# Moving a query scale into the softmax: eight short exponentials per tile on ScalarE

## The chip, the cores and the metric

The kernel runs on one core of a Trainium2 chip. The core has five engines with a queue each: TensorE (PE, matrix products; PEld are its weight loads), VectorE (DVE), ScalarE (ACT), GpSimd (POOL) and SyncE (SP, which only issues DMAs here). Each takes its instructions in order and waits on semaphores for the others. The time is that of one launch on the device, in microseconds (us); the median of several runs is compared.

## The reference

Four stages, each with a layernorm and a residual: a state-space layer ("mamba"), a routed expert layer, a dynamic convolution, and six layers of a local-attention transformer with a feed-forward part. Input is 4 sequences of 1024 tokens, 128 wide, float32. The change lies in the attention:

```python
q = l2norm(q) * qs
k = l2norm(k) * ksc
q = q * cos * scale + rotate_half(q) * sin * scale
k = k * cos * inv + rotate_half(k) * sin * inv
...
sim = jnp.einsum('bhwie,bhwje->bhwij', bq, bk2) * QK_SCALE
sim = jnp.where(mask, -jnp.finfo(sim.dtype).max, sim)
attn = jax.nn.softmax(sim, -1)
out = jnp.einsum('bhwij,bhwje->bhwie', attn, bv2)
```

There are 16 heads of 64; a window of 32 queries looks at 64 keys (its own window and the one before). `l2norm` divides a head's vector by its length. Since that is one number per query and head, it can be applied to the vector or, later, to the row of scores.

## The kernel before, in words

The transformer works on tiles of 128 tokens: 4 sequences, 6 layers, 8 tiles each, 192 in all. The loop in `Transformer.run` (L1501) takes one tile per turn and lists several parts of neighbouring tiles in it: the scores of tile i, the mixing of tile i - 1, the projection of tile i + 2 and a step of a feed-forward, beside steps of the first three stages for later sequences.

`project` (L1256) makes queries and keys of a tile. Four products of 512 columns go to PSUM banks named `qk`; ScalarE squares them, VectorE multiplies by cosine (to `r`) and by sine (to `rb`) and sums the squares. GpSimd adds `rb` to `r`. From the sums of squares `inverse_root` (L559) makes `root`, one over the length, for 16 query heads and 16 key heads; its helper operands are kept in `words`, a PSUM bank. Then, in L1296 to L1302, GpSimd multiplies `r` by `root`, first for the queries and then for the keys.

`turn` (L1314) transposes both on TensorE. `scores` (L1328) fills two banks named `sim`, one with the scores of the even heads (e = 0) and one of the odd heads, 8 heads x 64 keys each. The mask is put into the bank ahead of them, as 0 or -1e30. For each bank VectorE takes the row maximum `mx` and writes score minus maximum to `at` in SBUF, which empties the bank. One ScalarE exponential of 1024 columns covers both; VectorE sums, and GpSimd divides. `mix` (L1387) transposes the weights (`aT`), multiplies with the tokens (`zT`), and with the value and output weights (`wvo`).

The order on every engine is computed ahead by a planner, `Order.arrange` (L278). Each call is recorded in `take` (L170) as a unit with an engine, an estimated cost (`length`, L248) and its dependencies; a `together` block makes one unit of several calls at a given cost, so that nothing comes between. `arrange` gives out the unit that can start first, and among those of one engine that could start within a small tolerance (`NEAR`, 0.25 us for ScalarE) the one listed first. It chooses among 7 banks, held from the unit that first writes to the last that reads. A unit whose activation table differs from the last one costs 1.28 us more. For VectorE operations with two SBUF inputs (`both`, L196) there is a rule:

```python
                    if u.both:
                        t = max(t, clock["gpsimd"])
                    elif e == "gpsimd":
                        t = max(t, locked)
```

In the plan, such an operation starts when GpSimd has ended what it has been given, and GpSimd's next one waits for it. All instructions are issued from one helper, `give` (L369), so that the profile puts them at line 374: they are told apart by the names of their tiles.

Of the kernel before, what the change touches and what calls it, by code (L numbers as in the profile page):

```python
# [10 lines left out]
F32 = mybir.dt.float32  # L11
BF16 = mybir.dt.bfloat16
I32 = mybir.dt.int32
AF = mybir.ActivationFunctionType
ALU = mybir.AluOpType
AX = mybir.AxisListType
PSUM = bass.MemoryType.PSUM

P = 128
# [38 lines left out]
class Late:  # L58
# [4 lines left out]
    def __init__(self, bank, make=lambda ap: ap):  # L63
        self.bank, self.make = bank, make
# [80 lines left out]
class Order:  # L145
# [16 lines left out]
    def bank(self, name):  # L162
        return Late(Bank(self.psum[0], name))

    def together(self, cost):
        return Together(self, cost)

# [218 lines left out]


class Together:  # L390
    def __init__(self, order, cost):
        self.order, self.cost = order, cost

    def __enter__(self):
        o = self.order
        o.open = Unit("tensor", len(o.units))
        o.open.side = o.side
        o.units.append(o.open)
        o.forced = self.cost
# [750 lines left out]
class Transformer:  # L1150
# [4 lines left out]
    def __init__(self, ctx, c):  # L1155
        self.c, self.nc, self.io = c, c.nc, c.io
        one = self.sb = c.sb
        self.mask = one.tile([P, 2, 64], BF16, name="mask")
        self.identb = one.tile([P, P], BF16, name="identb")
        self.lng = one.tile([P, DEPTH], F32, name="lng")  # L1160
        self.lnb = one.tile([P, DEPTH], F32, name="lnb")
        self.b1 = one.tile([P, 2, 3, DEPTH], F32, name="b1")
        self.b2 = one.tile([P, DEPTH], F32, name="b2")
        self.maskf = one.tile([P, 2, 64], F32, name="maskf", tag="exsT", bufs=2)
        self.wvod = [c.dram.tile([P, 2, 8, D], F32, name=f"wvod{l}") for l in range(DEPTH)]
        self.rotd = [c.dram.tile([P, TPB, 4, DH], F32, name=f"rotd{l}") for l in range(DEPTH)]
        self.w, self.rot = {}, {}

    def prepare(self):

# [85 lines left out]
    def project(self, i, b, t):  # L1256

        nc, c = self.nc, self.c
        lhs = c.hs[b][0][:, PRE + t * P : PRE + (t + 1) * P]
        full, half = [P, HEADS, DH], [P, HEADS // 2, DH]  # L1260
        rs = []
        rot = self.rot.pop(i)
        w = c.tiny()
        ss = w[:, :32]
        for s in range(2):
            r = self.sb.tile(full, F32, "r", tag=f"r{s}", bufs=2)
            rb = self.sb.tile(full, F32, "rb", bufs=2)
            for j in range(2):
                hd = slice(8 * j, 8 * j + 8)
                ps = c.bank("qk")  # L1270
                nc.tensor.matmul(
                    ps, lhs, self.w["qk", s][:, j * 512 : (j + 1) * 512], start=True, stop=True
                )
                pv = ps.rearrange("p (h d) -> p h d", d=DH)
                sq = self.sb.tile(half, F32, "sq", bufs=2)
                nc.scalar.activation(sq, pv, AF.Square)
                cos, sin = rot[:, 2 * s, None, :], rot[:, 2 * s + 1]
                nc.vector.tensor_tensor(
                    out=r[:, hd, :], in0=pv, in1=cos.to_broadcast(half), op=ALU.mult
                )  # L1280
                nc.vector.tensor_tensor(
                    out=rb[:, hd, :].rearrange("p h (k d) -> p h k d", k=2),
                    in0=swapped(ps),
                    in1=sin.rearrange("p (k d) -> p k d", k=2)[:, None].to_broadcast(
                        [P, HEADS // 2, 2, DH // 2]
                    ),
                    op=ALU.mult,
                )
                c0 = s * HEADS + 8 * j
                nc.vector.tensor_reduce(out=ss[:, c0 : c0 + 8], in_=sq, op=ALU.add, axis=AX.X)  # L1290
            nc.gpsimd.tensor_tensor(out=r, in0=r, in1=rb, op=ALU.add)
            rs.append(r)
        root = self.sb.tile([P, 32], F32, "root", bufs=3)
        nc.vector.tensor_scalar(root, ss, 1e-24, None, ALU.max)
        c.inverse_root(root, root, w[:, 32:])
        for s in range(2):  # L1296
            nc.gpsimd.tensor_tensor(
                out=rs[s],
                in0=rs[s],
                in1=root[:, s * HEADS : (s + 1) * HEADS, None].to_broadcast(full),  # L1300
                op=ALU.mult,
            )  # L1302
        return rs

    def keys(self, prev_k):
# [19 lines left out]
                nc.scalar.copy(dst[:, 4 * j : 4 * j + 4, :], pt)  # L1325
        return qT

    def scores(self, t, qT, kT):  # L1328

        nc, c = self.nc, self.c
        m = self.mask[:, 0 if t == 0 else 1, None, :].to_broadcast([P, 8, 2 * WIN])
        sv = [c.bank("sim").rearrange("p (a k) -> p a k", k=2 * WIN) for e in range(2)]
        with nc.together(2.0):
            for e in range(2):
                nc.tensor.matmul(
                    sv[e], self.identb, m, start=True, stop=False, skip_group_check=True
                )
            for a in range(8):  # L1340
                for g in range(4):
                    for e in range(2):
                        rows = slice(e * 64, (e + 1) * 64)
                        cols = slice(g * WIN, (g + 1) * WIN)
                        nc.tensor.matmul(
                            sv[e][cols, a, :],
                            qT[rows, a, cols],
                            kT[rows, a, g * WIN : (g + 2) * WIN],
                            start=False,
                            stop=True,  # L1350
                            skip_group_check=True,
                        )
        mx = self.sb.tile([P, 2, 8], F32, "mx", bufs=3)
        at = self.sb.tile([P, 8, 2, 2 * WIN], F32, "at", bufs=2)
        for e in range(2):
            nc.vector.tensor_reduce(out=mx[:, e, :], in_=sv[e], op=ALU.max, axis=AX.X)
            nc.vector.tensor_tensor(
                out=at[:, :, e, :],
                in0=sv[e],
                in1=mx[:, e, :, None].to_broadcast([P, 8, 2 * WIN]),  # L1360
                op=ALU.subtract,
            )
        av = at.rearrange("p a e k -> p (a e) k")
        nc.scalar.activation(av, av, AF.Exp)
        sm = self.sb.tile([P, HEADS], F32, "sm", bufs=3)
        nc.vector.tensor_reduce(out=sm, in_=av, op=ALU.add, axis=AX.X)
        nc.vector.reciprocal(sm, sm)
        nc.gpsimd.tensor_tensor(
            out=av, in0=av, in1=sm[:, :, None].to_broadcast([P, HEADS, 2 * WIN]), op=ALU.mult
        )  # L1370
        return at
# [129 lines left out]
    def run(self):  # L1501
# [44 lines left out]
        kT = self.keys(None)  # L1546
        at = xw = None
        coming = going = None
        for i in range(len(tiles) + 4):
            mixing = iter(())  # L1550
            if i < len(tiles):
                b, l, t = tiles[i]
                qT = self.turn(projected.pop(i), kT)
            if going and going[4] == 1:
                next(going[0])
            if 0 < i <= len(tiles):
                bm, lm, tm = tiles[i - 1]
                mixing = self.mix(bm, tm, at, xw if tm else None)
                xw = next(mixing)
            along(i, 0.25)  # L1560
            second = going and going[4] == 1
            if going:
                next(going[0])
            if i < len(tiles):
                at = self.scores(t, qT, kT)
                kT = self.keys(kT if t + 1 < TPB else None)
            if second:
                next(going[0], None)
                bf, jf, lf = going[1:4]
                if lf == DEPTH - 1:  # L1570
                    self.output(bf, jf)
                if jf == BPB - 1 and i < len(tiles):
                    self.load_ffn((lf + 1) % DEPTH)
            along(i, 0.5)
            next(mixing, None)
            if going and not second:
                next(going[0])
            along(i, 0.75)
            if not second:
                ahead(i + 2)  # L1580
            next(mixing, None)
            if second:
                ahead(i + 2)
                going = None
            elif going:
                next(going[0])
                going[4] = 1
            if 0 < i <= len(tiles):
                if tm == TPB - 1 and i < len(tiles):
                    self.load_vo((lm + 1) % DEPTH)  # L1590
                if tm % 4 == 3:
                    going = [self.feedforward(bm, tm // 4, lm), bm, tm // 4, lm, 0]
            along(i, 1)
# [137 lines left out]
```

## Time and profile before

| | |
|---|---|
| median of 3 runs (lowest to highest) | 4260.55 us (4259.56 to 4266.35) |
| the profiled execution: time, span | 4259.06 us, 4257.2 us |
| mean granted TensorE clock | 0.948 of full speed |
| VectorE `at<-bank,mx`, 128x512, 384 times | 682 ns each, 254.6 us |
| VectorE sum `sm<-at`, 128x1024, 192 times | 1211 ns each, 232.5 us |
| GpSimd `r<-r,rb`, 128x1024, 384 times | 2367 ns each, 906.9 us |
| GpSimd `at<-at,sm`, 128x1024, 192 times | 1903 ns each, 365.4 us |
| ScalarE copy `zT<-bank`, 128x512, 768 times | 597 ns each, 403.7 us |
| ScalarE table loads, 195 times | 1283 ns each, 250.2 us |

A row of the groups reads: line, engine, operation, written tile <- read tiles, shapes, number | busy us in all, mean ns of one | idle us of that engine just before them, and what ended most of it. A row of waits reads: who waited <- for whom: us in all, times, longest. Busy shares are means over stretches with different limits; the slices show where each engine is full. A busy TensorE isn't TensorE at its peak: the ends of its products are modelled.

### The profile page before, as it was taken

To read this page: it belongs to the slowest core of one execution; us is meant where nothing else is said; L and a number is where in the kernel's file an instruction comes from. 1 tells how busy PE (TensorE), PEld (TensorE's weight loads), DVE (VectorE), ACT (ScalarE), POOL (GpSimd) and SP (SyncE) were. 2 spreads that over 40 slices of the span, in tenths; PEclk is the share of its full clock that TensorE was granted. 3 is DMA by queue.
4 is the path that set the end of the run, shared out by engine and by line. 5 is a ranking of instruction groups with operands and counts; after the bars stand their busy time and mean duration, and the time that the engine had idled before them with its cause. 6 is when DMAs were issued, how large, how long until landed. Compare 5 with 4: busy or idle time off the path is not lost. (4 is left out here: it accounts for less than half of the span.)

```text
span 4257.2 us, 112033 instructions
## 1 busy us (share of the span) xinstructions
PE 3801.6 (89%) x45306; PEld 2721.5 (64%) x45317; DVE 3612.4 (85%) x9374; ACT 2610.7 (61%) x4854; POOL 2964.5 (70%) x1832
## 2 busy tenths in 40 slices
PE   3874788998988999988999999999999999999997
PEld 1762465675665666656676677766666777777775
DVE  4668789888997879999998787898989898888985
ACT  3754466675555777655667676666665666666664
POOL 3388667666878766777789665788688666666663
PEclk6886899999998999989999999999999999999998
DMA  3323321222112221111113122121111010101100
GB/s 91 104 83 123 119 85 43 86 62 72 60 68 82 91 73 55 45 57 53 44 63 114 58 65 63 41 73 59 58 61 51 27 41 25 32 21 34 33 27 11
DMA packets 136878, 261.25 MB, mean 61 GB/s; under 512 B 16112, under 2 KB 93992, under 8 KB 129192
## 3 DMA queue, kind: packets, MB, share of 16 engines
q1 hardware_dynamic: 123352, 211.47, 15.0%
q0 software_dynamic: 13008, 42.62, 3.2%
q8 instruction: 357, 5.85, 0.6%
q14 instruction: 161, 1.32, 0.1%
HBM read 224.41 MB, written 29.62 MB: 60 GB/s over the span
## 5 line engine op out<-in xcount | busy, mean ns | idle before, releaser
L374 POOL TENSOR_TENSOR r<-r,rb 128x1024 f32<-128x1024 f32 x384 | 906.9, 2367 | 365.2 <-DVE rb L374 297.9
L374 POOL TENSOR_TENSOR r<-r,root 128x1024 f32<-128x1024 f32 x384 | 723.2, 1903 | 181.2 <-DVE root L374 154.4
L374 PE MATMUL bank<-wqk,hs 128*128 128x512 f32 x1536 | 769.7, 624 | 45.0 <-DVE at L374 13.3
L374 PEld LDWEIGHTS bank<-zT,wvo 128*128 128x128 f32 x6144 | 723.2, 194 | 88.8 <-issue 53.2
L374 PE MATMUL bank<-zT,wvo 128*128 128x128 f32 x6144 | 729.4, 277 | 6.5 <-ACT zT L374 3.5
L374 ACT ACTIVATE sq<-bank 128x512 f32<-128x512 f32 x768 | 450.4, 601 | 458.1 <-DVE words L374 228.1
L374 ACT COPY zT<-bank 128x512 f32<-128x512 f32 x768 | 403.7, 597 | 382.4 <-PE bank L374 376.6
L374 DVE TENSOR_TENSOR r<-bank,rot 128x512 f32<-128x512 f32 x768 | 522.0, 680 | 103.4 <-issue 36.2
L374 POOL TENSOR_TENSOR at<-at,sm 128x1024 f32<-128x1024 f32 x192 | 365.4, 1903 | 326.2 <-DVE sm L374 146.3
L374 DVE TENSOR_TENSOR rb<-bank,rot 128x512 f32<-128x512 f32 x768 | 520.8, 678 | 62.8 <-ACT sq L374 53.8
L374 DVE TENSOR_REDUCE words<-sq 128x8 f32<-128x512 f32 x768 | 526.5, 686 | 14.3 <-ACT sq L374 5.3
L374 PEld LDWEIGHTS bank<-wqk,hs 128*128 128x128 f32 x1536 | 267.6, 195 | 322.7 <-issue 157.7
L374 PE MATMUL bank<-aT,xw 64*128 64x256 f32 x3072 | 430.6, 404 | 25.4 <-DVE at L374 10.3
L374 PE MATMUL bank<-ident,r 128*128 128x128 f32 x3080 | 400.6, 278 | 45.1 <-DVE rb L374 10.0
L374 PEld LDWEIGHTS bank<-ident,r 128*128 128x128 f32 x3080 | 350.1, 143 | 134.9 <-issue 59.7
L374 PEld LDWEIGHTS bank<-aT,xw 64*128 64x128 f32 x3072 | 295.6, 192 | 153.2 <-issue 44.3
L374 PEld LDWEIGHTS bank<-kT,qT 64*32 64x32 f32 x24576 | 259.7, 106 | 106.8 <-issue 105.4
L374 PE MATMUL bank<-kT,qT 64*32 64x64 f32 x24576 | 296.6, 227 | 12.4 <-issue 11.9
L374 DVE TENSOR_REDUCE mx<-bank 128x8 f32<-128x512 f32 x384 | 254.1, 680 | 44.4 <-PE bank L374 44.3
L374 PE MATMUL bank<-fxn,w 128*128 128x512 f32 (+1 forms) x576 | 272.8, 607 | 7.0 <-ACT fxn L374 4.8
L374 ACT ACTIVATE at<-at 128x1024 f32<-128x1024 f32 x192 | 203.5, 1060 | 117.6 <-DVE at L374 83.2
L374 ACT COPY qT<-bank 128x512 f32<-128x512 f32 x384 | 228.3, 600 | 66.2 <-PE bank L374 62.8
(207 smaller groups left out, 6849.8 us busy)
## 6 DMA issues: line engine op xcount, KB each, us to landing
near<-rows SPq DMA_DIRECT2D x31, 1024.0 KB
near<-rows SPq DMA_DIRECT2D x31, 960.0 KB
rot<-rotd SPq DMA_DIRECT2D x192, 128.0 KB
wqk<-in_Wqkv SPq DMA_DIRECT2D x48, 512.0 KB
wvo<-wvod SPq DMA_DIRECT2D x24, 1024.0 KB
ewt<-in_w_ex SPq DMA_DIRECT2D x16, 514.0 KB
w<-in_W SPq DMA_DIRECT2D x24, 341.0 KB
wvod<-eT SPq DMA_DIRECT2D x24, 256.0 KB
```

What stands on the lines that cost most here:

```text
L374: getattr(engine, op)(*map(real, args), **{k: real(v) for k, v in kw.items()})
```

## The change

The queries of the even heads are no longer multiplied by their root. GpSimd multiplies only the odd query heads and all key heads. In the softmax of the even heads VectorE takes the maximum of the unscaled scores and makes minus maximum times root from it; ScalarE then computes exp(root x score - root x maximum) straight from the bank, one instruction of 64 columns per head, with root as its scale and the product as its bias. The eight are listed as two units of four, each booked at 1.12 us. The odd heads keep their subtraction and get an exponential of their own, of 512 columns. The ring of root tiles grows from 3 to 5.

```diff
-    def together(self, cost):
-        return Together(self, cost)
+    def together(self, cost, engine="tensor"):
+        return Together(self, cost, engine)
...
 class Together:
-    def __init__(self, order, cost):
-        self.order, self.cost = order, cost
+    def __init__(self, order, cost, engine):
+        self.order, self.cost, self.engine = order, cost, engine
...
-        o.open = Unit("tensor", len(o.units))
+        o.open = Unit(self.engine, len(o.units))
...
-        self.w, self.rot = {}, {}
+        self.w, self.rot, self.roots = {}, {}, {}
...
-        root = self.sb.tile([P, 32], F32, "root", bufs=3)
+        root = self.sb.tile([P, 32], F32, "root", bufs=5)
         nc.vector.tensor_scalar(root, ss, 1e-24, None, ALU.max)
         c.inverse_root(root, root, w[:, 32:])
-        for s in range(2):
-            nc.gpsimd.tensor_tensor(
-                out=rs[s],
-                in0=rs[s],
-                in1=root[:, s * HEADS : (s + 1) * HEADS, None].to_broadcast(full),
-                op=ALU.mult,
-            )
+
+        qo = rs[0].rearrange("p (a e) d -> p a e d", e=2)[:, :, 1, :]
+        ro = root[:, :HEADS].rearrange("p (a e) -> p a e", e=2)[:, :, 1:2]
+        nc.gpsimd.tensor_tensor(
+            out=qo, in0=qo, in1=ro.to_broadcast([P, HEADS // 2, DH]), op=ALU.mult
+        )
+        nc.gpsimd.tensor_tensor(
+            out=rs[1], in0=rs[1], in1=root[:, HEADS:, None].to_broadcast(full), op=ALU.mult
+        )
+        self.roots[i] = root
         return rs
...
-    def scores(self, t, qT, kT):
+    def scores(self, i, t, qT, kT):
...
-        for e in range(2):
-            nc.vector.tensor_reduce(out=mx[:, e, :], in_=sv[e], op=ALU.max, axis=AX.X)
-            nc.vector.tensor_tensor(
-                out=at[:, :, e, :],
-                in0=sv[e],
-                in1=mx[:, e, :, None].to_broadcast([P, 8, 2 * WIN]),
-                op=ALU.subtract,
-            )
+        even = self.roots.pop(i)[:, :HEADS].rearrange("p (a e) -> p a e", e=2)[:, :, 0]
+        nc.vector.tensor_reduce(out=mx[:, 0, :], in_=sv[0], op=ALU.max, axis=AX.X)
+        nc.vector.scalar_tensor_tensor(mx[:, 0, :], mx[:, 0, :], -1.0, even, ALU.mult, ALU.mult)
+        for a0 in (0, 4):
+            with nc.together(1.12, "scalar"):
+                for a in range(a0, a0 + 4):
+                    nc.scalar.activation(
+                        at[:, a, 0, :],
+                        sv[0][:, a, :],
+                        AF.Exp,
+                        bias=mx[:, 0, a : a + 1],
+                        scale=even[:, a : a + 1],
+                    )
+        nc.vector.tensor_reduce(out=mx[:, 1, :], in_=sv[1], op=ALU.max, axis=AX.X)
+        nc.vector.tensor_tensor(
+            out=at[:, :, 1, :],
+            in0=sv[1],
+            in1=mx[:, 1, :, None].to_broadcast([P, 8, 2 * WIN]),
+            op=ALU.subtract,
+        )
+        nc.scalar.activation(at[:, :, 1, :], at[:, :, 1, :], AF.Exp)
         av = at.rearrange("p a e k -> p (a e) k")
-        nc.scalar.activation(av, av, AF.Exp)
```

More of the change, by code (lines that the diff above doesn't have):

```diff
@@ L1564, in run @@
             if i < len(tiles):
-                at = self.scores(t, qT, kT)
+                at = self.scores(i, t, qT, kT)
                 kT = self.keys(kT if t + 1 < TPB else None)
```

## The prediction

> **What bounds the kernel now.** I read the page's busy line first, then its slices, then the groups of the softmax, then what TensorE waited for, and last the order of time around one softmax.
>
> ```profile
> PE 3801.6 (89%) x45306; PEld 2721.5 (64%) x45317; DVE 3612.4 (85%) x9374; ACT 2610.7 (61%) x4854; POOL 2964.5 (70%) x1832
> ...
> PE   3874788998988999988999999999999999999997
> ...
> DVE  4668789888997879999998787898989898888985
> ACT  3754466675555777655667676666665666666664
> PEclk6886899999998999989999999999999999999998
> ```
>
> TensorE is busy for 89% of the span, but not evenly. Summing the stretches: from 0 to 532 us it is busy 338.3 us (start-up), from 532 to 3325 us 2569.8 of 2793 (92%), from 3325 to 4123 us 784.2 of 798 (98%). After 532 us only 262 us of TensorE idle are left. Any gain must come out of them; a loss has no such cap. What ended these waits, from 532 us to the end:
>
> ```profile
> PE bank L374 <- DVE at L374: 37.0, 37, 5.2
> PE bank L374 <- DVE rb L374: 28.5, 35, 4.9
> PE bank L374 <- ACT fxn L374: 24.8, 28, 4.5
> ...
> PE bank L374 <- ACT qT L374: 13.6, 21, 1.4
> ...
> PE bank L374 <- ACT zT L374: 12.6, 24, 1.2
> ...
> PE bank L374 <- POOL r L374: 7.1, 8, 2.4
> ```
>
> Added up by engine: VectorE 129 us, ScalarE 79 us, GpSimd 13 us. The first two rows are PSUM banks that TensorE wanted back: `at` is the subtraction that empties a score bank, `rb` the rotation that empties a projection bank.
>
> **The change, part by part.** A tile is 128 tokens; there are 192. The rows as they stand now:
>
> ```profile
> L374 POOL TENSOR_TENSOR r<-r,root 128x1024 f32<-128x1024 f32 x384 | 723.2, 1903 | 181.2 <-DVE root L374 154.4
> ...
> L374 DVE TENSOR_REDUCE mx<-bank 128x8 f32<-128x512 f32 x384 | 254.1, 680 | 44.4 <-PE bank L374 44.3
> ...
> L374 ACT ACTIVATE at<-at 128x1024 f32<-128x1024 f32 x192 | 203.5, 1060 | 117.6 <-DVE at L374 83.2
> ```
>
> GpSimd: half of the query multiply goes. The row is 1903 ns for 1024 columns; the same kind of multiply with 496 columns (`ew<-ew,csm`) took 1022 ns. So 1903 - 1022 = 0.88 us less per tile, 169 us in all. The chain of waits shows the query multiply and the key multiply in series ahead of the transposes, once per layer in the last stretch, but TensorE's whole wait for `r` is 7.1 us: worth at most that; I take 5 us. All else there is behind other work.
>
> VectorE: one subtraction of 682 ns goes, one `scalar_tensor_tensor` over 8 columns comes. Nearest row by size: the same operation on 4 columns takes 150 ns. That is a gain of 0.53 us per tile, 102 us, if nothing blocks it. But both its tensors (`mx` and the roots) lie in SBUF. The inverse root avoids this by keeping one operand in PSUM. What two SBUF inputs cost is in the trace, where the router's small operations meet GpSimd (order of time, start and length in us; first row GpSimd):
>
> ```profile
> 2138.38 4.71 POOL L374 TENSOR_TENSOR r<-r,rb 128x1024 f32<-128x1024 f32 x2
> ...
> 2141.11 2.06 DVE L374 TENSOR_TENSOR ehot<-rank,ebest 128x64 f32<-128x64 f32 x1
> ```
>
> The same operation takes 0.21 us when GpSimd is idle; here it ends at 2143.17, just after GpSimd's pair ends at 2143.09. The Trainium skill, page "SBUF — State Buffer", section "Who interferes with whom", has the rule: a VectorE instruction with two SBUF inputs takes a read port shared with GpSimd, and the later one is blocked for the whole instruction of the other. It speaks against this change. By the rule alone, an arrival at random finds GpSimd busy 0.65 of the time (0.70 less the part removed) with on average half of some 2 us left: 0.65 us, so VectorE would lose 0.65 - 0.53 = 0.12 us per tile. The measured row is nearer to a planned instruction:
>
> ```profile
> L374 DVE SCALAR_TENSOR_TENSOR m<-m,dpar,m 128x512 f32<-128x512 f32 x7 | 9.0, 1286 | 0.0
> ```
>
> Without contention it is 751 ns (its one twin on `r`), so the mean stall is 0.53 us, though the planner holds such an operation until its GpSimd clock is free, as it will the new one. Bounds: 0 and 2.37 us (the longest common GpSimd operation). I take 0.53: VectorE's gain is used up, 0 us. A blocked VectorE also holds up what is queued behind it: the reduction of the odd heads, and the rotations that empty projection banks.
>
> ScalarE: one exponential of 1060 ns goes; one of 512 columns and eight of 64 come. For 512 columns from SBUF the row `m<-m` gives 0.63 us. For 64 columns with scale and bias read per partition the nearest row is the layernorm:
>
> ```profile
> 3779.47 1.53 ACT L374 ACTIVATE fxn<-bank,mean,rs 128x128 f32<-128x128 f32 x4
> ```
>
> One of these lasts 463 ns on average, so the spacing is (1.53 - 0.46)/3 = 0.36 us. ScalarE's rows grow by 0.80 ns a column (`ehg`: 378 ns at 128, 481 at 256), so 64 columns less save 0.05: 0.41 us long, 0.305 apart. Eight in a row: 7 x 0.305 + 0.41 = 2.55 us. Cheapest end: the spacing of `ehg`, with only a bias to read, (1.15 - 0.38)/3 - 0.05 = 0.21, so 1.8 us. Dearest: no overlap, 8 x 0.41 = 3.3 us. The middle one has the same operands and stands. Sum: 2.55 + 0.63 - 1.06 = +2.1 us per tile, 407 us in all; ScalarE goes from 2611 to 3018 us. The planner books 2 x 1.12 = 2.24 us for the eight, 0.3 us too little, so all behind them on ScalarE comes later than planned. There are 195 table loads of 1283 ns; the exponentials are now three units per tile instead of one, and a gelu may be put between them. Bounds 0 and 48 more (one per feed-forward, 62 us of ScalarE); I take none.
>
> What 407 us of ScalarE cost TensorE: from 532 us on, ScalarE's share goes from 2353/3725 = 0.63 to 0.74, and TensorE's waits for it are 79 us. Bounds: if waits grow with the share, 79 x (0.74/0.63 - 1) = +14 us; if they grow as in a queue fed at random, by share/(1 - share), 1.7 to 2.8, +51 us. The order is planned, not random, and TensorE has other tiles to turn to: I take +25 us, nearer to the first. Behind the exponentials on ScalarE are the copies of `zT` (2.06 us for four), of `qT`, `kT` and the squares; TensorE's output product waits for the first.
>
> The bank: the even score bank is now emptied at 0.68 + 0.15 + 0.53 + 2.55 = 3.9 us after the first reduction starts instead of 1.4, and later if the copies of `zT` go first, as they do at 3740.81 in the trace. The odd bank comes free no later than before. Of the 37 waits on `at`, call half the even bank's: 18. Bounds: 0 if another bank serves, 18 x 2.5 = 45 us if none does. I take 12 us, since seven banks turn over and only two are score banks.
>
> The deeper ring of roots costs nothing: no wait on a root buffer is in the trace.
>
> Sum: -5 (GpSimd) + 0 (VectorE) + 25 (ScalarE waits) + 12 (bank) = +32, less some 5 us because the odd bank is free about half a microsecond sooner in the rest of those waits (19 x 0.53 is 10, half of it taken). That is +27 on the profiled execution's 4259.06 us: 4286 us. The median of the runs, 4260.55, is 1.5 us from it; I leave that difference alone.
>
> **Rivals.** *VectorE's relief decides* (faster). In ten of the 133 us stretches after 532 us VectorE is busy 90% or more, and TensorE is idle for 103 us of them. At one tile per 20.4 us (192 from 300 to 4210) they hold some 65 tiles: 65 x 0.53 = 34 us, if the small operation isn't blocked. With the lower bound of ScalarE's waits, +14, it makes -20: 4239 us. It decides if the stall is near zero and the bank isn't missed. For it: VectorE's waits are the largest sum. Against: `m<-m,dpar,m`.
>
> *ScalarE stands in TensorE's way in every tile* (slower by more). Scores have a lower index than the same turn's `zT` copies, so where both are ready within 0.25 us the planner puts exponentials first, up to 1.12 us at a time. If half of one such unit reaches TensorE in each tile, 192 x 0.5 = 96 us: 4355 us. For it: the last stretch has only 1.7% idle to hide it in. Against: waits for `zT` are 12.6 us now in 192 tiles.
>
> *All is absorbed*: the planner finds another order, losses and gains stay within 9 us, 4260 us. That the edit doesn't do what it says I don't count: the multiply and the subtraction are gone from the code.
>
> **Chances and range.** Forecast (+9 to +60 us, 4268 to 4320) 0.45; VectorE's relief 0.25 (4215 to 4252); ScalarE in the way 0.15 (4320 to 4400); absorbed 0.15, of which 0.02 falls on the slower side. A difference under 0.2%, 8.5 us, can't be told from none here. So faster 0.25, same 0.13, slower 0.62. The range 4232 to 4345 takes in the forecast and the absorbed case (0.60), most of the relief (0.18) and a third of the worse case (0.05): 0.83. The likeliest case's own range is 4268 to 4320.
>
> **What would show it.** GpSimd's `r<-r,root` for queries near 1.0 us; VectorE's new row well above 0.15 us, with lengths that end where a GpSimd operation ends; eight ScalarE rows near 0.41 us, 0.3 apart, ScalarE near 3018 us; TensorE's waits on ScalarE up from 79 us to about 104, with waits on the even bank now put down to ScalarE's `at`. I am wrong if the new VectorE row stays at 0.15 and VectorE's waits fall, or if ScalarE's waits don't rise.

## The result and the profile after

The changed kernel takes 4438.89 us (median of 3 runs, 4436.81 to 4443.12) against 4260.55: ratio 1.0424, 95% interval [1.0407, 1.0441], 178 us slower. The forecast was 4286 us, with a range to 4345. The direction was right and the size wrong by a factor of six to seven (178 us for 27).

The page after, busy line and the slices of TensorE and ScalarE with the granted clock:

```profile
PE 3872.4 (87%) x45317; PEld 2736.5 (62%) x45317; DVE 3634.2 (82%) x9374; ACT 2975.1 (67%) x6401; POOL 2804.4 (63%) x1832
...
PE   3865788998888899887999999998998999999997
...
ACT  3653566776566787755667788766666776777775
PEclk6886799999999999988999999999998999999998
```

The span is 4437.0 us. ScalarE's busy time grew by 364 us (407 estimated), GpSimd's fell by 160 (169 estimated), VectorE's rose by 22 (0 estimated). TensorE has the same instructions; its idle time grew by 109 us and its rows by 71, at a mean clock of 0.939 instead of 0.948. The loss isn't in one place: from the 25th tile to the last, every stretch of 24 tiles takes 9 to 31 us longer than before (counted from the end of one tile's division to the end of another's).

The rows that the change made, from the groups with shapes kept apart:

```profile
L374 ACT ACTIVATE at<-bank,mx,root 128x64 f32<-128x64 f32 x1536 | 474.9, 415 | 110.7 <-DVE mx L374 103.6 <-DVE words L374 5.0 <-PE bank L374 0.8
...
L374 ACT ACTIVATE at<-at 128x512 f32<-128x512 f32 x192 | 125.5, 654 | 54.4 <-DVE at L374 32.1 <-DVE ne L374 9.7 <-DVE words L374 6.2
...
L374 POOL TENSOR_TENSOR r<-r,root 128x512 f32<-128x512 f32 x192 | 201.3, 1048 | 148.3 <-DVE root L374 138.7 <-DVE rs L374 3.0 <-DVE mx L374 1.8
...
L374 DVE SCALAR_TENSOR_TENSOR mx<-mx,root 128x8 f32<-128x8 f32 x192 | 94.7, 493 | 0.1
```

All four are within 0.2 us of the prices in the prediction (the largest difference is the last row's, 0.49 us for 0.68). So the operations were priced about rightly, and what they do to others was not. What TensorE waited for, longest first:

```profile
PE bank L374 <- ACT at L374: 81.5, 89, 7.1
PE bank L374 <- DVE m L374: 70.0, 55, 11.4
PE bank L374 <- POOL at L374: 39.2, 16, 14.0
```

The first row is new. All of it is ended by the exponentials of 64 columns, and the products that wait don't read `at`: they wait for the even score bank, which these exponentials read. The third row was 8.6 us before:

```profile
PE bank L374 <- POOL at L374: 8.6, 12, 2.5
```

Added up over all rows of this view, the waits on ScalarE went from 200 to 304 us, on GpSimd from 18 to 45, on VectorE from 184 to 173.

The order of time shows the longest of the first row's waits:

```profile
1439.41 4.64 POOL L374 TENSOR_TENSOR r<-r,rb 128x1024 f32<-128x1024 f32 x2
...
1440.04 6.13 DVE L374 SCALAR_TENSOR_TENSOR mx<-mx,root 128x8 f32<-128x8 f32 x1
...
1444.03 2.11 POOL L374 TENSOR_TENSOR near<-near,ew 128x1024 f32<-128x1024 f32 x1
1446.20 2.47 ACT L374 ACTIVATE at<-bank,mx,root 128x64 f32<-128x64 f32 x8 [5.41 <-DVE mx L374]
...
1448.72 1.69 PE L374 MATMUL bank<-aT,xw 64*128 64x256 f32 x5 [7.07 <-ACT at L374]
```

An operation on 8 columns lasts 6.13 us. It ends at 1446.17, just after the third GpSimd operation in a row (1444.03 + 2.11 = 1446.14). VectorE does nothing else in that time. The eight exponentials start when it ends, and TensorE waits 7.07 us for them.

### The profile page after: what moved, and what is told of

It is laid out like the page before. It is cut to its first block, busy times and chain, and to the rows that moved or that the text cites. A ratio compares the mean times of both kernels' runs of the same rounds, so it can differ in the third digit from the quotient of the medians.

```text
span 4437.0 us, 113616 instructions
## 1 busy us (share of the span) xinstructions
PE 3872.4 (87%) x45317; PEld 2736.5 (62%) x45317; DVE 3634.2 (82%) x9374; ACT 2975.1 (67%) x6401; POOL 2804.4 (63%) x1832
## 4 chain that ended last, share of the span: by engine, by line
PE 25%; DVE 23%; ACT 10%; issue 4%; POOL 2%; DMA 0%; ACTq 0%; POOLq 0%; DVEq 0%
PE bank L374 25%; DVE words L374 5%; ACT at L374 4%; DVE r L374 4%; DVE rb L374 4%; DVE mx L374 3%; DVE ne L374 2%; DVE sm L374 2%; ACT sq L374 2%; ACT zT L374 1%; DVE hs L374 1%; DVE at L374 1%; ACT fxn L374 1%; ACT qT L374 1%; DVE st L374 1%
## 5 line engine op out<-in xcount | busy, mean ns | idle before, releaser
L374 PE MATMUL bank<-wqk,hs 128*128 128x512 f32 x1536 | 789.5, 633 | 61.3 <-ACT at L374 19.4
L374 POOL TENSOR_TENSOR r<-r,root 128x512 f32<-128x512 f32 (+1 forms) x384 | 558.5, 1475 | 148.3 <-DVE root L374 138.7
L374 ACT COPY zT<-bank 128x512 f32<-128x512 f32 x768 | 413.0, 610 | 218.8 <-PE bank L374 212.0
L374 ACT ACTIVATE at<-bank,mx,root 128x64 f32<-128x64 f32 x1536 | 474.9, 415 | 110.7 <-DVE mx L374 103.6
L374 PEld LDWEIGHTS bank<-ident,r 128*128 128x128 f32 x3080 | 359.2, 145 | 211.3 <-issue 131.4
L374 PE MATMUL bank<-aT,xw 64*128 64x256 f32 x3072 | 447.3, 410 | 42.8 <-ACT at L374 11.7
L374 PE MATMUL bank<-ident,r 128*128 128x128 f32 x3080 | 421.7, 282 | 69.6 <-ACT at L374 30.6
L374 ACT ACT_TABLE_LOAD x206 | 264.3, 1283 | 107.4 <-DVE mx L374 91.5
L374 PE MATMUL bank<-fxn,w 128*128 128x512 f32 (+1 forms) x576 | 282.9, 616 | 17.3 <-ACT fxn L374 8.0
```

The lines of the kernel that those rows point to most:

```text
L374: getattr(engine, op)(*map(real, args), **{k: real(v) for k, v in kw.items()})
```

## The experiments

All are compared with the kernel before, run beside them on the same chip. Ratios are used, since that kernel's median differed from call to call (4261.07, 4249.95 and 4248.88 us).

**The maximum in PSUM.**

```diff
-        nc.vector.tensor_reduce(out=mx[:, 0, :], in_=sv[0], op=ALU.max, axis=AX.X)
-        nc.vector.scalar_tensor_tensor(mx[:, 0, :], mx[:, 0, :], -1.0, even, ALU.mult, ALU.mult)
+        top = c.tiny()[:, :8]
+        nc.vector.tensor_reduce(out=top, in_=sv[0], op=ALU.max, axis=AX.X)
+        nc.vector.scalar_tensor_tensor(mx[:, 0, :], top, -1.0, even, ALU.mult, ALU.mult)
```

> The changed kernel, but the maximum of the even heads goes to the PSUM tile of small words, so that the product with the roots has only one SBUF input; nothing else differs. Port theory (the VectorE operation with two SBUF inputs, blocked by GpSimd and in the plan held back to GpSimd's clock, makes the loss): the row mx<-words,root falls from 493 to about 155 ns and the time to under 4320 us. ScalarE theory (2.1 us more ScalarE work per tile makes the loss) and bank theory (the even score bank is held until eight exponentials are done): VectorE gets 65 us back, and the time stays at 4400 us or more.

4360.06 us, 1.0234 [1.0217, 1.0251]. From the groups and the waits of this run:

```profile
L374 DVE SCALAR_TENSOR_TENSOR mx<-words,root 128x8 f32<-128x8 f32 x192 | 30.3, 158 | 0.8
...
PE bank L374 <- ACT at L374: 44.2, 56, 3.0
```

The row fell from 493 to 158 ns, 64 us in all, and the time by 79 us: 1.9 of the 4.2 per cent. Each theory named a part and neither the whole; 2.3 per cent remain. TensorE's waits for the exponentials fell from 81.5 to 44.2 us, and those for GpSimd's `at` from 39.2 to 10.0.

**The split exponentials alone**, in the kernel before (the remaining 512 columns follow as one):

```diff
-        nc.scalar.activation(av, av, AF.Exp)
+        for a0 in (0, 4):
+            with nc.together(1.12, "scalar"):
+                for a in range(a0, a0 + 4):
+                    nc.scalar.activation(
+                        at[:, a, 0, :],
+                        at[:, a, 0, :],
+                        AF.Exp,
+                        bias=self.none[:, a : a + 1],
+                        scale=c.one8[:, a : a + 1],
+                    )
+        nc.scalar.activation(at[:, :, 1, :], at[:, :, 1, :], AF.Exp)
```

> The kernel before, but the one exponential of 1024 columns is split as the change splits it: eight of 64 columns with scale (ones) and bias (zeros) read per partition, from the subtracted scores in SBUF, and one of 512. Both banks are emptied by VectorE as before, and GpSimd's work is as before. ScalarE theory: 4380 us or more (most of the +178). Port theory and bank theory: 4260 to 4300 us.

4394.98 us, 1.0318 [1.0300, 1.0335]. The port theory, as the whole cause, falls here: VectorE and GpSimd have the instructions of before, and 3.2 per cent are lost. TensorE's longest wait is a new one:

```profile
PE bank L374 <- ACT zT L374: 107.1, 108, 4.0
```

The order of time in the last stretch shows how it comes about:

```profile
3594.85 1.07 ACT L374 COPY zT<-bank 128x512 f32<-128x512 f32 x2 [2.31 <-PE bank L374]
...
3596.73 2.76 ACT L374 ACTIVATE at<-at,none,one 128x64 f32<-128x64 f32 x8 [0.80 <-DVE at L374]
...
3599.40 0.61 ACT L374 ACTIVATE at<-at 128x512 f32<-128x512 f32 x1
3599.92 1.04 ACT L374 COPY zT<-bank 128x512 f32<-128x512 f32 x2
3600.62 0.63 PE L374 MATMUL bank<-ident,r 128*128 128x128 f32 x4 [1.51 <-ACT zT L374]
```

The four `zT` copies of a tile are cut in two with 3.3 us of exponentials between them, after a wait of 0.80 us for VectorE's subtraction. TensorE waits 1.51 us until one of the last two copies is done. Counted over the trace, the exponentials that lie between the first and the last of a tile's four copies take 288 us here and 46 us in the kernel before.

**The same, with the bank held.** The even heads' subtraction is written back to the score bank and read from there:

```diff
-                out=at[:, :, e, :],
+                out=sv[0] if e == 0 else at[:, :, e, :],
...
-                        at[:, a, 0, :],
+                        sv[0][:, a, :],
```

> As the run with the split exponentials, but the even heads' subtraction is written back into the score bank and the eight exponentials read it there: the same ScalarE count, VectorE and GpSimd as before, and the bank held until ScalarE is done, as in the change. Bank theory: 60 us or more above the run with the split exponentials. ScalarE theory: within 25 us of it. Port theory: both under 4300 us.

4351.40 us, 1.0214 [1.0197, 1.0231]: 1.04 points less than with the bank set free early. That is the other way than the bank theory had it, and more than the 25 us that the ScalarE theory allowed. TensorE's waits:

```profile
PE bank L374 <- ACT at L374: 61.8, 74, 2.6
...
PE bank L374 <- ACT zT L374: 28.6, 64, 3.8
```

TensorE does wait for the held bank, 61.8 us, but its waits for `zT` fell from 107.1 to 28.6. So the bank as the cause of the loss is refuted; a small cost of holding it is not, because more than the bank differs. The exponentials are shorter from the bank (415 ns for 428), so that ScalarE is busy for 37 us less, and the plan has another order. At the 0.3 us found below for each us of ScalarE, the 37 us are worth 11 of the 44 us (an estimate). Why this order is the better one was not tried.

**Booked at what they measure**: `nc.together(1.30, "scalar")` in place of 1.12.

> The changed kernel with each unit of four exponentials booked at 1.30 us, near what it measures, instead of 1.12. If the loss comes from a plan that runs ahead of ScalarE, the time falls below 4400 us; under the ScalarE, bank and port theories it stays within 25 us of 4439.

4461.29 us, 1.0473 [1.0456, 1.0491], half a per cent slower than the change. Under-booking isn't the cause.

**Doses.** Two exponentials of 512 columns from SBUF instead of one of 1024:

```diff
-        nc.scalar.activation(av, av, AF.Exp)
+        nc.scalar.activation(at[:, :, 0, :], at[:, :, 0, :], AF.Exp)
+        nc.scalar.activation(at[:, :, 1, :], at[:, :, 1, :], AF.Exp)
```

> The kernel before with its one exponential of 1024 columns split in two of 512 (even and odd heads), both from SBUF: +0.2 us of ScalarE per tile, 13 of the +134 us that the split into eight and one cost. If ScalarE's time makes the loss (dose theory): 4261 to 4285 us. If splitting as such does it, since the plan is rearranged and table loads move (order theory): 4330 us or more.

And as in the split above, with `at[:, a : a + 2, 0, :]` at every second a, and 0.62 us booked for two:

> As the run with eight exponentials from SBUF, but with four of 128 columns (two heads each): about half of the added ScalarE time, some +1.1 us per tile. Dose theory: about half of the +134 us, 4310 to 4345 us. Order theory: as with eight, 4380 us or more.

4266.69 us, 1.0041 [1.0027, 1.0055], and 4319.10 us, 1.0163 [1.0143, 1.0184]. Beside ScalarE's busy time over that of before (2610.7 us):

| even heads' exponentials | ScalarE, us more | time |
|---|---|---|
| one of 512 | 9 | +0.4% |
| four of 128 | 203 | +1.6% |
| eight of 64 | 392 | +3.2% |

From the first row to the last, 2.8 per cent (118 us) for 383 us of ScalarE: 0.3 us of time for each. The dose theory held and the order theory, that any split costs the full sum, fell. All three keep the usual place in the list, so that more ScalarE time also means more of it ahead of the copies; the runs listed late part the two.

**Controls for the plan.** The same instructions as before, the exponential booked at 1.06 us:

> A control: the kernel before with the same instructions, only the exponential of 1024 columns booked in the plan at 1.06 us, as it measures, instead of 0.97. It shows how far the time moves because the plan is another one: within 15 us of 4261 if the plan's noise is small against the steps of the other runs, over 40 us away if it isn't.

4261.85 us, 1.0034 [1.0024, 1.0044]: within the 15 us named. And the kernel before with its exponential listed behind the `zT` copies (the edit of the next run, without the rest):

> A control: the kernel before with the exponential, the sum and the division listed behind the same turn's zT copies. With one exponential of 1.06 us there is little to be put ahead of the copies: within 20 us of the kernel before. If late listing is good as such, 4230 us or less.

4282.05 us, 1.0073 [1.0056, 1.0090], 33 us, outside the 20 us named. Another plan for the same instructions moves the time by 0.3 to 0.7 per cent, so steps of that size between runs have no cause that can be named here. The granted clock moves with it: 0.945 and 0.944 on average in these two, 0.949 in the kernel before beside each.

**Listed late.** The run with the maximum in PSUM, with `scores` in two parts (the odd heads' maximum and subtraction go to the first):

```diff
+        yield at
         for a0 in (0, 4):
...
             next(mixing, None)
+            if i < len(tiles):
+                next(softmax)
```

> As the run with the maximum in PSUM (4360 us), but the exponentials, the sum and the division are listed behind the same turn's zT copies, so that the planner prefers the copies where both can start. If the loss that remains comes from exponentials put ahead of the copies that TensorE waits for: 4310 us or less. If it is ScalarE's time as such: within 25 us of 4360.

4294.00 us, 1.0107 [1.0089, 1.0126], against 1.0234 in the usual place: as the order explanation expected. The split exponentials from SBUF, listed late in the same way:

> As the run with eight exponentials from SBUF (3.2% over the kernel before), listed behind the zT copies. If its loss is mostly exponentials put ahead of the copies: under 1.5% over the kernel before, with TensorE's waits for zT well under the 107 us of that run. If it is ScalarE's time as such: 2.5% or more.

4328.47 us, 1.0183 [1.0166, 1.0200], against 1.0318. The threshold of 1.5 per cent was not reached, nor the 2.5 of the other side. TensorE waits less for the copies, and for other things in their place:

```profile
PE bank L374 <- DVE at L374: 42.7, 34, 7.7
...
PE bank L374 <- ACT zT L374: 31.4, 47, 1.6
```

So listing them late takes back 1.35 of 3.18 points from SBUF and 1.27 of 2.34 with the maximum in PSUM: that much goes with their place in the list, ahead of copies that TensorE needs. The edit does what it was meant to do: the exponentials between a tile's copies come down from 288 to 69 us in all, and from 243 to 56. What is left over the late control (0.73) is 1.1 points from SBUF, and with the maximum in PSUM 0.3, which is within the plan's noise.

**The plan's holding back.** The changed kernel, with the planner's rule for two SBUF inputs not applied to this operation:

```diff
-                len([a for a in ins if free_size(a) > 1]) > 1
+                len([a for a in ins if free_size(a) > 1]) > 1 and free_size(out) != 8
```

> The changed kernel, but the planner's rule for two SBUF inputs isn't applied to the 8-column operation; the instruction itself is the same and GpSimd can still block it. If the loss from the port is the plan's holding back (79 us between the change and the run with the maximum in PSUM), the time falls to about 4360 us although the row mx<-mx,root gets longer than 493 ns. If it is the blocking on the chip, the time stays at 4420 us or more.

4418.37 us, 1.0400 [1.0383, 1.0418]; the row rises from 493 to 643 ns:

```profile
L374 DVE SCALAR_TENSOR_TENSOR mx<-mx,root 128x8 f32<-128x8 f32 x192 | 123.4, 643 | 0.1
```

Of the 1.9 points 1.7 stay, so it is the blocking on the chip more than the rule in the plan. Without the rule there is also more blocking, so the two can't be parted further. The expectation's 4420 was missed by 2 us, with the time still 58 us above the other theory's value.

**The relief alone.** The run with the maximum in PSUM, with one exponential for the even heads in place of the eight. It takes the first head's scale and bias for all, and so leaves the other heads' own scales out:

```diff
+        nc.scalar.activation(
+            at[:, :, 0, :], sv[0], AF.Exp, bias=mx[:, 0, :1], scale=even[:, :1]
+        )
```

> As the run with the maximum in PSUM, but one exponential of 512 columns for the even heads, with the first head's scale and bias for all of them, instead of eight of 64: it changes the weights of seven heads and leaves ScalarE's added work out, so that only the relief of VectorE (one subtraction per tile) and GpSimd (half a multiply) is left. If the relief is worth something by itself: 4200 to 4240 us. If neither engine set the end: within 15 us of 4255.

4271.12 us, 1.0054 [1.0038, 1.0071], 16 us from the 4255 named, where 15 were allowed. The page's busy line and the waits for the even bank:

```profile
PE 3823.4 (90%) x45317; PEld 2717.6 (64%) x45317; DVE 3572.9 (84%) x9374; ACT 2646.8 (62%) x5054; POOL 2808.7 (66%) x1832
...
PE bank L374 <- ACT at L374: 34.0, 43, 3.8
```

GpSimd is relieved of 156 us and VectorE of 40 and ScalarE has 36 us more, and nothing is gained. So with nearly all of ScalarE's added work gone the change would have brought nothing, up to the plan's noise. TensorE waits 34.0 us for the even bank here at hardly any loss: a sum of waits is not a loss by itself.

The total divides into steps between runs: 0.5 points up to the relief alone (within the plan's noise), 1.8 from there to the maximum in PSUM (seven more exponentials on ScalarE), 1.9 from there to the change (the shared port). Each step carries the plan's noise of 0.3 to 0.7 points. No run was faster than the kernel before, and none points to a version that would be: what the change gives back is worth nothing here.

## Why the prediction was wrong, by its steps

Two steps failed. The stall of the small operation was entered as 0 us and cost 79. ScalarE's added work was entered as 37 us (25 for waits, 12 for the bank) and cost 1.8 points, 77 us. The 0.5 points of the relief alone are within the plan's noise. The direction was not luck, since ScalarE's added work was named as the loss; its size was wrong.

- *GpSimd, -5 us; VectorE, 0 us.* The busy times are about right (-160 and +22 us). The relief is worth nothing (the relief alone).
- *The small operation, 0.15 + 0.53 us: "VectorE's gain is used up".* It measured 0.49. The step that failed is that its stall was entered as VectorE time that cancels a saving. In the order of time above it is a delay in a chain: the exponentials, the sum, GpSimd's division and TensorE's transposes all come behind it. With the stall gone, the time fell by 79 us and the waits for the exponentials by 37. The upper bound of 2.37 us, one GpSimd operation, was wrong too: the longest was 6.13.
- *ScalarE's waits, +25 us, "the order is planned, not random, and TensorE has other tiles to turn to"; the bank, +12 us.* From 532 us on, TensorE's waits on ScalarE rose from 79 to 186 us, and not to 104. Of the 186, 80 are waits for the even bank, and the other 106 are near the 104. By the rows, then, it is the bank that was sized wrongly (18 waits and 12 us were put down for it, 45 at most). But the rows don't say what an earlier free bank would save. From SBUF, with the bank free early, the waits for `zT` came in their place and the time was longer; with the relief alone there were 34 us of bank waits at hardly any loss. What failed in both terms is that waits of the kernel before were scaled or counted. What counted was where the new work went: ahead of copies that empty banks (listing it late takes back 1.27 points), and into a bank that TensorE wants back.
- *The rival "ScalarE stands in TensorE's way in every tile", 4355 us.* This was one of the two mechanisms, priced at 96 us against some 77 measured. It was given 0.15. What spoke against it, that waits for `zT` were only 12.6 us, said nothing on what happens once something else is put between the copies.
- *VectorE's relief, 4239 us.* Refuted by the relief alone.
- *Table loads, none more.* There are 206 for 195, 14 us of ScalarE: right to a small difference.
- The forecast took one loss at a time. The range ended where either of the two large ones would have ended alone; they came together.
- TensorE's own rows, 71 us longer, were not in the sum. The granted clock explains about half (3802 x (0.948/0.939 - 1) = 36 us, an estimate); the rest was not separated, nor why the clock is lower.

## What to carry to other kernels

An engine that is 61% busy isn't 39% free if it also empties the banks of the engine that sets the end: price new work on it by what it is put in front of, copy by copy, in the tightest stretch, and by the bank that it reads. A stall of an in-order engine is to be entered as a delay of all that follows it in its chain, and not as busy time that a saving elsewhere pays for. Before moving work off an engine, ask what TensorE's waits on that engine would be worth if the work were simply gone; here a run without it gained nothing.

## What the runs showed of the hardware

- A VectorE operation with two SBUF inputs that meets GpSimd can stay blocked for longer than one GpSimd operation. Of the 192 in the changed kernel, 48 lasted over 0.25 us; 47 of them ended 20 to 37 ns after the end of a GpSimd operation. Of these, 40 ended behind the first one that they met and 7 behind the second or third. Where the next GpSimd operation followed at once, VectorE was let in 12 times and passed over 9 times. The Trainium skill, page "SBUF — State Buffer", section "Who interferes with whom", has the lock held for one whole instruction; the trace agrees on the lock, and shows that a waiting VectorE can be passed over at the boundary. What decides it the trace does not show.
- Where the exponential was split, table loads took over waits of the first exponential. ScalarE's idle time before table loads was 4.1 us in the kernel before and 107.4 in the changed one, 78.6 with two exponentials:

```profile
L374 ACT ACT_TABLE_LOAD x195 | 250.2, 1283 | 4.1 <-PEq L1719 0.7
...
L374 ACT ACT_TABLE_LOAD x206 | 264.3, 1283 | 107.4 <-DVE mx L374 91.5 <-DVE at L374 12.1 <-PEq L1734 0.7
```

The load's 1.28 us then comes after the data is ready and not beside the wait. With two exponentials the time was only 0.4 per cent up, and 0.5 in the relief alone, where this idle time was 104.6 us, so it is a small part.
